# Four graph and expert layers on one core: bias vectors as bf16 parts, the weight ring ahead of the dispatch, choice by logits, an adjacency normalisation in attention

## The chip, the cores and the metric

The kernel runs on one core of a Trainium2 chip. A core has a matrix engine (PE, with its weight loads shown apart as PEld), a vector engine (DVE), a scalar engine (ACT), a general engine (POOL) and a queue engine for transfers (SP); each takes its instructions in order, and they meet through semaphores. The metric is the device time of one execution in microseconds (us), taken as the median of several runs.

## The reference

Four layers, each a graph convolution and a mixture of experts, act on 625 nodes with 512 features and 10,000 edges. Each half adds its result to x, and reads the normalised x:

```python
x = x + _L0_gnn_ref(_layernorm(x), edge_index, ...)   # mean over neighbours, two products, batch norm
x = x + _L0_ffn_ref(_layernorm(x)[None], ...)         # attention, then 8 experts of 128 hidden, all weighted
x = x + _L1_gnn_ref(_layernorm(x), edge_index, ...)   # two rounds of attention over the edges
x = x + _L1_ffn_ref(_layernorm(x)[None], ...)         # top 2 of 8 experts, 1024 hidden
x = x + _L2_gnn_ref(_layernorm(x), edge_index, ...)   # bases, mixed by weights of each node
x = x + _L2_ffn_ref(_layernorm(x)[None], ...)         # 8 experts of 128 hidden, two weights not zero
x = x + _L3_gnn_ref(_layernorm(x), edge_index, ...)   # one normalised convolution, gelu
x = x + _L3_ffn_ref(_layernorm(x)[None], ...)         # top 2 of 8 gated experts, 1536 hidden
```

What the change touches in it: an expert's output is `h @ W2[e] + b2[e]`, weighted by the node's gate, so the biases of all experts add `comb @ b2` (nodes x 8 times 8 x 512). Layer 1 chooses by logits and takes a softmax over the two chosen ones; layer 3 takes a softmax over all eight, the top two of it, and divides both by their sum. Layers 2 and 3 weigh each edge with `dinv[src] * dinv[dst]`, where `dinv` is one over the root of the degree.

## The kernel before

Nodes lie in NT = 5 tiles of T = 125, features in KD = 4 groups of 128. Matrix products are in float32, which the profile shows as two records each; one-hots and counts are fp16. The framework places instructions on each engine's queue and adds waits by its own reading of the dependencies; tiles of a closed pool give their addresses to the next, whose writers then wait for the last users.

**Setup.** The matrix of edge counts is a product of one-hots: for each of 80 groups of 125 edges, DVE makes `src` and `dst` (L911, L913) and PE adds five products into `ps_a` (L916). It is done in three parts of 27, 27 and 26 groups. After each part ACT casts `ps_a` to integers `v` (L929), DVE splits them into digits (L934, L936), and in the first part the layer norm `xn` is computed (L277 to L303), turned to features `xnT` (L328, L226), and added to x by POOL (L946). The four `ps_a`-sized PSUM buffers are shared by all this. The expert vectors `b2s` (8 rows of 3 x 512) and two rows of constants `cbs` are loaded there by SP.

**Weights** come as chunks of 1 MB, issued by SP at L206: three at a time through `take` for most stages, and through a ring of 11 in the routed experts (three of `take`'s buffers, five of a pool opened there, three of the pool `T` of feature tiles).

**Small experts** (layers 0 and 2, `small_experts`): two experts' hidden parts (`ahead`, `ps_mf`, L359) go first, then the bias product (`expert_bias`: five transposes L479, copies of the turned weights L481 and L482, five products `ps_eb` L486, each added to x by DVE), and then, expert by expert, the next hidden part and the outputs (`ps_eo`, L496).

**Routed experts** (layers 1 and 3): the normed rows go to DRAM (`rows_out`, L511), logits give the two chosen experts of each node (`top2`), `dispatch` gives every chosen pair a place in a block of 128 rows of one expert, by prefix sums on PE and one-hot products, and so the list `node` of the rows of each block (L584) and later the `gate` of each row (L615). `routed` then opens the ring, gathers each block's rows by an indirect DMA on POOL (`fetch`, L667), turns them (L674), multiplies by the expert's first weights (`ps_h`; L1170 in layer 1, L1335 in layer 3), turns the hidden part (L688) and multiplies by the second weights (`ps_y`, L697); the result is weighted (L703) and added into DRAM by an indirect DMA (L705). A list `fill` gives small tasks to slip between the units: in layer 1 the bias product, the keeping of x, and the steps of `normalise` (L1195), which turns the edge counts into the normalised adjacency that layers 2 and 3 use. The ring's first 11 chunks are asked for in `refill()`, after the dispatch in the program.

**Attention of layer 1** runs two rounds `l`; each makes q, k and v from three chunks of weights and then calls `attention`, where ACT, DVE and POOL work on 625-wide rows of scores (L796 to L860).

**Layer 2's convolution** adds, in the product `pr` of each of five node tiles, the rows `cbs` by a two-row product with ones.

Of the kernel before, what the change touches and what calls it, by code (L numbers as in the profile page):

```python
# [10 lines left out]
F32 = mybir.dt.float32  # L11
# [7 lines left out]
P = 128  # L19
# [133 lines left out]
def kernel(  # L153
# [29 lines left out]
    b2s = const.tile([34, 3, D], F32, name="b2s")  # L183
    cbs = b2s[32:34, 0, :]
# [287 lines left out]
    def expert_bias(comb, b2):  # L472

        cT = small.tile([P, NP], F32, tag="lg_T", name="cT", bufs=1)[:E]

        def turned():
            ps = pstile("ps_eb")
            for t in range(NT):
                nc.tensor.transpose(ps[:E, t // 4, t % 4 * T:(t % 4 + 1) * T], comb[:, t, :],  # L479
                                    ident[:T, :T])  # L480
            nc.scalar.copy(cT[:, :4 * T], ps[:E, 0, :4 * T])  # L481
            nc.vector.tensor_copy(cT[:, 4 * T:N], ps[:E, 1, :T])  # L482

        def added(t):
            ps = pstile("ps_eb")
            nc.tensor.matmul(ps[:T, 0, :], cT[:, t * T:(t + 1) * T], b2, start=True, stop=True)  # L486
            nc.vector.tensor_add(x[:, t, :], x[:, t, :], ps[:T, 0, :])

        return [turned] + [lambda t=t: added(t) for t in range(NT)]
# [24 lines left out]
    def dispatch(layer, o12, weight, w0, per):  # L514


        with tc.tile_pool(name=f"{layer}d", bufs=1) as dp:
# [12 lines left out]
            for s in range(NT):  # L530
                nc.tensor.matmul(tot, ones16, mask[:, s, :], start=(s == 0), stop=(s == NT - 1))
            gt = dp.tile([P, E, 4], F32, tag="gt", name="gt")
# [30 lines left out]
            ohp = dp.tile([T, 2 * NT, B], BF16, tag="ohp", name="ohp")  # L563
            ohb = dp.tile([T, 2 * NT, NB], F32, tag="ohb", name="ohb")
            nc.vector.tensor_tensor(ohb, blk[:T, None, :].to_broadcast([T, 2 * NT, NB]),
                                    bcast(at[:, 1, :], NB), op=OP.is_equal)
            nums = dp.tile([T, 2 * NT, NB, 2], BF16, tag="nums", name="nums")
            num = number.rearrange("p c t i -> p (c t) i")
            for i in range(2):
                nc.vector.tensor_mul(nums[:, :, :, i], ohb, bcast(num[:, :, i], NB))  # L570
            ps = pstile("ps_id")
            for n in range(2 * NT):
                nc.vector.tensor_scalar(ohp[:, n, :], place[:T, :], at[:, 0, n:n + 1], None,
                                        op0=OP.is_equal)
                nc.tensor.matmul(ps[:, 0, :2 * NB], ohp[:, n, :],
                                 nums[:, n].rearrange("p b i -> p (b i)"), start=(n == 0),
                                 stop=(n == 2 * NT - 1))
            one = dp.tile([P, NB], F32, tag="one", name="one")
            nc.vector.tensor_reduce(one, ps[:, 0, :2 * NB].rearrange("p (b i) -> p b i", i=2),
# [170 lines left out]
    def small_experts(src, comb, b1, b2, hpool, ln):  # L750
# [12 lines left out]
        for e in range(2):  # L763
            ahead(e)
# [615 lines left out]
```

## Time and profile before

| what | us |
|---|---|
| median of three runs | 1726.1 |
| lowest and highest | 1724.55, 1726.1 |
| the profiled execution | 1723.04 |
| its span | 1721.1 |
| PE busy in it | 1528.4 |
| DVE busy | 676.1 |
| ACT busy | 357.8 |
| POOL busy | 235.5 |

The page gives the share of busy time of each engine in 40 equal slices of the span, then the transfers, then the chain of work that ended last, then the costliest groups of instructions. A digit of the slices is tenths; the row PEclk is the clock granted to PE in tenths of full speed, and its mean over the span is 0.936. Where a line is followed by a bracket, it says how long the engine was idle before it and what released it. A group of one line and one form reads like this: the line, the engine, the operation, the tiles written and read, partitions x elements of each, how many, busy time and mean duration in ns, and the idle time before:

```profile
L1335 PE MATMUL ps_h<-ring,xgT 128*128 128x512 f32 x624 | 274.8, 595 | 0.8 <-DVE xgT L226 0.8
L825 POOL TENSOR_SCALAR s<-s,rs 125x625 f32<-125x625 f32 (+4 forms) x120 | 103.2, 875 | 294.0 <-DVE rs L822 269.9
```

The first is the largest product of the kernel, 624 records that hardly ever wait. The second is an operation that is often idle for the engine ahead of it.

### The profile page before, as it was taken

The page shows a single profiled execution, that of the slowest core. Times are in us where ns is not written, and L with a number is a line of the kernel's source. Part 1 is how long each engine was busy: PE and PEld are TensorE (multiplying, and loading weights), DVE is VectorE, ACT ScalarE, POOL GpSimd, SP SyncE. Part 2 cuts the span into 40 slices and gives each one's busy share as a digit, 9 for nine tenths or more (in the row PEclk, how much of TensorE's full clock was granted, in tenths as well). Part 3 has the DMA queues.
Part 4 walks back from the last instruction along what each step waited for, and adds up shares of the span by engine and source line. Part 5 has one row for each costly group of instructions (what it writes and reads, how often), then busy time and mean ns, then how long its engine had stood idle before and what let it go on. Part 6 is the DMA issues. An engine that isn't in the chain of part 4 may idle for free.

```text
span 1721.1 us, 15559 instructions
## 1 busy us (share of the span) xinstructions
PE 1528.4 (89%) x5642; PEld 861.3 (50%) x5642; DVE 676.1 (39%) x1738; ACT 357.8 (21%) x680; POOL 235.5 (14%) x254
## 2 busy tenths in 40 slices
PE   7996999989897989846999969698759999999997
PEld 5774466555555656533444436354534444444443
DVE  9824562451974168466122225635331111111110
ACT  1102362011661046311111115301211000000100
POOL 2010042010540034101111112001000000000000
PEclk8998999999999989977999989799869999999998
DMA  3000200011001100136889731011258888869871
GB/s 135 16 28 25 73 1 25 31 68 53 22 1 49 49 26 1 40 112 234 302 270 342 256 87 73 25 49 49 102 217 299 301 309 304 307 244 359 311 265 50
DMA packets 40142, 237.12 MB, mean 138 GB/s; under 512 B 4779, under 2 KB 4907, under 8 KB 14299
## 3 DMA queue, kind: packets, MB, share of 16 engines
q1 hardware_dynamic: 30705, 214.80, 33.7%
q0 software_dynamic: 6608, 15.99, 4.1%
q10 hardware_dynamic: 2746, 5.25, 1.0%
q8 instruction: 48, 0.79, 0.2%
q14 instruction: 35, 0.29, 0.1%
HBM read 246.11 MB, written 14.26 MB: 151 GB/s over the span
## 4 chain that ended last, share of the span: by engine, by line
PE 70%; DVE 12%; issue 10%; DMA 4%; ACT 2%; POOL 1%; SPq 0%; POOLq 0%; ACTq 0%; DVEq 0%
PE ps_mf L359 17%; PE ps_y L697 9%; PE ps_h L1335 9%; PE ps_mn L367 7%; PE ps_h L1170 5%; PE ps_s L796 4%; PE ps_eo L496 4%; PE ps_o L860 3%; DMA sumsL<-slots,node 3%; PE ps_p L839 3%; PE ps_tr L328 2%; DVE ln_st L277 1%; DVE s L802 1%; PE ps_t L688 1%; DVE dst L913 1%
## 5 line engine op out<-in xcount | busy, mean ns | idle before, releaser
L1335 PE MATMUL ps_h<-ring,xgT 128*128 128x512 f32 x624 | 274.8, 595 | 0.8 <-DVE xgT L226 0.8
L697 PE MATMUL ps_y<-ring,hT 128*128 128x512 f32 x536 | 239.2, 593 | 0.9 <-issue 0.9
L1335 PEld LDWEIGHTS ps_h<-ring,xgT 128*128 128x128 f32 x624 | 118.7, 191 | 147.9 <-issue 145.3
L697 PEld LDWEIGHTS ps_y<-ring,hT 128*128 128x128 f32 x536 | 97.6, 190 | 103.9 <-issue 103.0
L825 POOL TENSOR_SCALAR s<-s,rs 125x625 f32<-125x625 f32 (+4 forms) x120 | 103.2, 875 | 294.0 <-DVE rs L822 269.9
L705 POOL DMA_INDIRECT sumsL<-slots,node x27 | 42.6, 1578 | 469.3 <-DVE slots L703 358.6
L1338 ACT ACTIVATE g<-ps_h 128x512 f32<-128x512 f32 x39 | 23.3, 597 | 395.6 <-PE ps_h L1335 364.5
L1170 PE MATMUL ps_h<-ring,xgT 128*128 128x512 f32 x224 | 103.2, 609 | 2.1 <-ACT xgT L234 1.3
L807 ACT ACTIVATE s<-s,mn 125x626 f32<-125x626 f32 (+4 forms) x120 | 87.2, 743 | 49.3 <-DVE mn L802 49.1
L802 DVE CUSTOM_DVE_ANT_0 s<-ps_s,mask 125x626 f32<-125x626 f32 (+4 forms) x120 | 82.6, 718 | 29.0 <-PE ps_s L796 27.8
L796 PE MATMUL ps_s<-kT,qT 64*125 64x313 f32 (+4 forms) x416 | 86.4, 466 | 2.8 <-DVE mn L802 2.8
L328 PE MATMUL ps_tr<-ident,xn 125*128 125x125 f32 x140 | 30.2, 398 | 62.6 <-DVE ln_nb L300 49.1
L226 DVE COPY hT<-ps_t 128x512 f32<-128x512 f32 x26 | 18.0, 692 | 171.5 <-PE ps_t L688 171.5
L1340 DVE TENSOR_TENSOR h<-ps_h,g 128x512 f32<-128x512 f32 x39 | 26.8, 686 | 147.9 <-ACT g L1338 147.9
L839 PE MATMUL ps_p<-ident,s 125*125 125x125 f32 x432 | 65.8, 293 | 14.0 <-POOL s L825 11.7
L359 PE MATMUL ps_mf<-xT,w 128*128 128x313 f32 x256 | 69.7, 434 | 6.6 <-ACT xT L402 6.6
L839 PEld LDWEIGHTS ps_p<-ident,s 125*125 125x125 f32 x432 | 53.9, 194 | 40.0 <-POOL s L825 28.6
L1170 PEld LDWEIGHTS ps_h<-ring,xgT 128*128 128x128 f32 x224 | 43.6, 196 | 57.5 <-issue 53.8
L817 DVE SCALAR_TENSOR_TENSOR s<-s,cnt 125x626 f32<-125x626 f32 x80 | 67.3, 863 | 9.9 <-ACT s L807 9.9
L496 PE MATMUL ps_eo<-w,h 128*125 128x512 f32 x160 | 70.6, 592 | 0.0
L860 PE MATMUL ps_o<-pT,v 125*64 125x375 f32 (+2 forms) x448 | 60.1, 413 | 9.0 <-DVE mn L802 4.2
L916 PE MATMUL ps_a<-dst,src 125*128 125x313 f16 x400 | 58.0, 309 | 6.9 <-DVE dst L913 5.3
(345 smaller groups left out, 1994.8 us busy)
## 6 DMA issues: line engine op xcount, KB each, us to landing
ring<-in_weights SPq DMA_DIRECT2D x195, 1024.0 KB
w<-in_weights SPq DMA_DIRECT2D x27, 1024.0 KB
rows_hbm<-xn ACTq DMA_DIRECT2D x2, 1120.0 KB
sumsL<-x ACTq DMA_DIRECT2D x2, 1120.0 KB
out<-sumsL SPq DMA_DIRECT2D x1, 1250.0 KB
x<-in_x SPq DMA_DIRECT2D x1, 1120.0 KB
x<-sumsL SPq DMA_DIRECT2D x5, 224.0 KB
rows<-in_rows SPq DMA_DIRECT2D x1, 1052.0 KB
```

The costliest lines, as they stand in the source:

```text
L359: nc.tensor.matmul(ps[:, half, :HC], w, r[:, half * HC:(half + 1) * HC], start=(n == 0), stop=(n == last))
L367: nc.tensor.matmul(ps[:T, 0, :width], src[:, k, t * T:(t + 1) * T], w[:, k, :width], start=(k == 0), stop=(k == KD - 1 and extra is None))
L496: nc.tensor.matmul(ps[:T, 0, :], h[:, t * T:(t + 1) * T], w, start=(f == 0), stop=(f == len(blocks) - 1))
L697: nc.tensor.matmul(ys[b][:, 0, :], hT[:, j, :], ring[n % RING][:, j, :], start=(c == 0 and j == 0), stop=(c == nch - 1 and j == 3))
L796: nc.tensor.matmul(ps[hh][:T, i, :w], qT[rr, b, t * T:(t + 1) * T], kT[rr, b, i * w:(i + 1) * w], start=True, stop=True)
L802: nc.vector.tensor_tensor_reduce(s[:, hh, :nb * w].rearrange("p (a c) -> p a c", a=nb), ps[hh][:T, :nb, :w], mask[:, t, :nb * w].rearrange ...
L807: nc.scalar.activation(s[:, hh, :nb * w], s[:, hh, :nb * w], AF.Exp, bias=mn[:, hh:hh + 1], scale=-1.0, accum_out=sm[:, hh:hh + 1] if caus ...
L825: nc.gpsimd.tensor_scalar(s[:, hh, :w], s[:, hh, :w], rs[:, hh:hh + 1], 1.0, op0=OP.mult, op1=OP.mult)
L839: nc.tensor.transpose(pp[:T, hh, j * T:(j + 1) * T], s[:, hh, j * T:(j + 1) * T], ident[:T, :T])
L860: nc.tensor.matmul(po[rr, 0, o:n * T], v[:, j, h * DH:(h + 1) * DH], pT[:, hh, j, o:n * T], start=(j == 0), stop=(j == nk - 1))
L1170: nc.tensor.matmul(ps[:, 0, :], xgT[:, k, :], w1[:, k, :], start=(k == 0), stop=(k == KD - 1))
L1335: nc.tensor.matmul(ps[:, i, :], xgT[:, k, :], w[i][:, k, :], start=(k == 0), stop=(k == KD - 1))
```

## The change

1. `b2s` becomes 72 rows of bf16: each float32 is held as three bf16 parts which add up to it, in three groups of rows, and each group is loaded in copies. `cbs` becomes six rows in the same way. A new helper `parted` builds both in setup: transfers on ACT's queue, then copies and masked activations on ACT and subtractions on POOL. The weights `comb` are split in three parts as well (`parts`, on POOL), so that one bf16 product of 72 rows stands for the float32 product of 8 rows. In `small_experts` the bias steps come inside the expert loop, after the third hidden part. In layer 2's convolution the two-row product becomes a six-row bf16 product.
2. `routed` makes the choice and the dispatch itself. Its pools are opened and the ring's 11 chunks are asked for before them, and the first two gathers are issued as soon as `node` is there.
3. The choice goes by logits in both routed layers, and the weight of a pair comes from the exponent of their difference (`choose`, `weigh`), computed after the prefix sums.
4. The number of a row is one fp16 value and not two bf16 parts, so that `nums` has 17 columns and not 34, and one reduction goes.
5. `normalise` is called in layer 1's second attention round, two steps after each group of q, k and v, and no longer in the routed experts' fill.

```diff
-    b2s = const.tile([34, 3, D], F32, name="b2s")
-    cbs = b2s[32:34, 0, :]
+    b2s = const.tile([9 * E, 3, D], BF16, name="b2s")
+    cbs = const.tile([6, D], BF16, name="cbs")
...
-    def expert_bias(comb, b2):
-        cT = small.tile([P, NP], F32, tag="lg_T", name="cT", bufs=1)[:E]
+    def expert_bias(comb, layer):
+        cT = small.tile([9 * E, NP], BF16, tag="cT", name="cT", bufs=1)
+        rest = stile("eb_r")
+        part = small.tile([T, NT, E], BF16, tag="eb_p", name="eb_p")
+        c9 = small.tile([T, NT, 3, 3, E], F32, tag="c9", name="c9", bufs=1)
+
+        def parts():
+            nc.gpsimd.tensor_copy(rest, comb)
+            for i in range(3):
+                nc.gpsimd.tensor_copy(part, rest)
+                if i < 2:
+                    nc.gpsimd.tensor_sub(rest, rest, part)
+                for j in range(3):
+                    nc.gpsimd.tensor_copy(c9[:, :, j, i, :], part)
...
-                nc.tensor.transpose(ps[:E, t // 4, t % 4 * T:(t % 4 + 1) * T], comb[:, t, :],
-                                    ident[:T, :T])
-            nc.scalar.copy(cT[:, :4 * T], ps[:E, 0, :4 * T])
-            nc.vector.tensor_copy(cT[:, 4 * T:N], ps[:E, 1, :T])
+                nc.tensor.transpose(ps[:9 * E, t // 4, t % 4 * T:(t % 4 + 1) * T],
+                                    c9[:, t].rearrange("p j i e -> p (j i e)"), ident[:T, :T])
+            nc.scalar.copy(cT[:, :4 * T], ps[:9 * E, 0, :4 * T])
+            nc.scalar.copy(cT[:, 4 * T:N], ps[:9 * E, 1, :T])
...
-            nc.tensor.matmul(ps[:T, 0, :], cT[:, t * T:(t + 1) * T], b2, start=True, stop=True)
+            nc.tensor.matmul(ps[:T, 0, :], cT[:, t * T:(t + 1) * T], b2s[:, layer, :], start=True,
+                             stop=True)
...
+    def choose(lg):
+        m1, m2, o12 = top2(lg)
+        g12 = small.tile([T, 2, NT], F32, tag="g12", name="g12")
+        def weigh():
+            nc.vector.tensor_sub(g12[:, 1], m2, m1)
+            nc.scalar.activation(g12[:, 1], g12[:, 1], AF.Exp)
+            nc.vector.tensor_scalar(g12[:, 0], g12[:, 1], 1.0, None, op0=OP.add)
+            nc.vector.reciprocal(g12[:, 0], g12[:, 0])
+            nc.vector.tensor_mul(g12[:, 1], g12[:, 1], g12[:, 0])
+        return o12, g12, weigh
...
-            for i in range(2):
-                nc.vector.tensor_mul(nums[:, :, :, i], ohb, bcast(num[:, :, i], NB))
+            nc.vector.tensor_mul(nums, ohb, bcast(number.rearrange("p c t -> p (c t)"), NB))
...
-            nc.vector.tensor_reduce(one, ps[:, 0, :2 * NB].rearrange("p (b i) -> p b i", i=2),
-                                    axis=AX.X, op=OP.add)
...
             nc.vector.scalar_tensor_tensor(node, one, -1.0, free, op0=OP.add, op1=OP.add)
+            fetch(node)
...
-            refill()
+            while brought["n"] < RING:
+                bring(brought["n"])
+                brought["n"] += 1
+            o12, g12, weigh = choose(lg)
+            gate, whose = dispatch(layer, o12, g12, weigh, w0, per, first_rows)
...
-        for step in expert_bias(comb, b2):
-            step()
         for e in range(E):
             if e + 2 < E:
                 ahead(e + 2)
+            for step in bias[3 * e:3 * e + 3]:
+                step()
...
+    def parted(dst, src, n, pool):
+        rows3, width = dst.shape
+        per = rows3 // 3
+        full = pool.tile([rows3, width], F32, name=f"full{n}")
+        for g in range(rows3 // n):
+            nc.scalar.dma_start(full[g * n:(g + 1) * n], src)
...
+        for j in range(2):
+            nc.scalar.copy(dst, full)
+            nc.scalar.activation(part, dst, AF.Copy, scale=off[:, j:j + 1])
+            nc.gpsimd.tensor_sub(full, full, part)
+        nc.scalar.copy(dst, full)
...
-                nc.sync.dma_start(b2s[:E], b2_in)
-                nc.sync.dma_start(cbs, cb_in)
+                parted(b2s.rearrange("p l d -> p (l d)"), b2_in, E, setup)
+                parted(cbs, cb_in, 2, setup)
...
         for l in range(2):
+            if l == 1:
+                normalise()
...
-            pr = mm_nodes(xnT, wres, t, extra=(ones[32:34, :T], cbs))
+            pr = mm_nodes(xnT, wres, t, extra=(ones16[:6, :T], cbs))
...
-    pr = softmax8(node_logits(xnT, vec("L3_ffn_router_w"), None, "lg"))
-    m1, m2, o12 = top2(pr)
...
-    node, gate, whose = dispatch("L3", o12, g12.rearrange("p c t -> p (c t)"), W_L3, 9)
+    lg = node_logits(xnT, vec("L3_ffn_router_w"), None, "lg")
```

## The prediction

> **What bounds the kernel now.** I read the page's shares and slices first, then the chain that ended last, then stretches of it.
>
> ```profile
> PE   7996999989897989846999969698759999999997
> DVE  9824562451974168466122225635331111111110
> PEclk8998999999999989977999989799869999999998
> PE 70%; DVE 12%; issue 10%; DMA 4%; ACT 2%; POOL 1%; SPq 0%; POOLq 0%; ACTq 0%; DVEq 0%
> ```
>
> PE is the bound: 89% busy and 70% of the chain. A slice is 43 us. The first, one with PE at 4, and some with a clock of 6 to 8 tenths are where something else decides, and these are where the change works. In the long stretches of 9 (expert blocks) it alters nothing, so I forecast only at the seams.
>
> Rows of the chain, then stretches (length; busy time of PE, PEld, DVE, ACT, POOL; clock; DMA share; GB/s):
>
> ```profile
> 299.73 6.53 PE ps_eb L486 x10
> 786.47 5.24 DMA slots<-rows_hbm,node
> 1112.96 7.38 PE ps_eb L486 x10
> 1272.42 7.72 DMA slots<-rows_hbm,node
> ```
>
> ```profile
> 298.00:306.20 8.20, 7.42 (x18) 2.62 (x16) 3.03 (x5) 1.23 (x2) 4.96 (x1) 0.75 0.00 1
> 1111.50:1120.30 8.80, 8.02 (x17) 2.85 (x15) 3.03 (x5) 1.23 (x2) 0.00 (x0) 0.67 0.01 2
> 1120.30:1126.80 6.50, 6.50 (x17) 4.42 (x17) 0.69 (x1) 0.00 (x0) 0.00 (x0) 0.66 0.00 0
> ```
>
> The 8-row fp32 bias products (L486) stand on the path three times, and with them the clock is about two thirds, also over the full-size matmuls just after; it is 1.00 in the stretch that follows each (311 to 316, 1126.8 to 1131). The two gathers are waited for bare.
>
> **1. Setup (`parted`): costs +9.** Setup's start, from the timeline:
>
> ```profile
> 27.46 7.38 POOL L946 TENSOR_TENSOR x<-x,xn 125x512 f32<-125x512 f32 x5 [17.92 <-DVE ln_nb L300]
> 29.24 1.55 DVE L934 TENSOR_SCALAR acc<-v 125x626 int32<-125x626 int32 x1
> 32.34 0.42 ACT L929 CAST v<-ps_a 125x313 int32<-125x313 f32 x1 [2.74 <-DVE acc L936]
> 32.82 1.10 PE L328 MATMUL ps_tr<-ident,xn 125*128 125x125 f32 x4 [2.06 <-ACT v L929]
> 36.29 24.00 PE L916 MATMUL ps_a<-dst,src 125*128 125x313 f16 x166 [1.59 <-DVE xnT L226]
> ```
>
> Until 25 DVE paces (20.00 us busy in 5 to 25, the one-hots); between the first and second part of the edge count PE waits for the norm, and resumes at 36.29. The change puts 12 DMA issues, a table load, six copies and four activations on ACT, and four subtractions on POOL, into this. Loads end at about 18 (DMA row), so `b2s`'s copies start about 11 to 17. What waits on ACT's in-order queue is behind all of them: the norm's root, `xn`, the casts `v`, so PE and DVE wait with it. The order built of the changed program has ACT: copies, two activations, root of the norm, two `v`, copies, activations, two `xn`, third copies, third `v`, `xnT`. Sizes: ACT copies 512 columns in 0.58 (rows of 128x512), so 1536 in about 1.7, and POOL adds 125x512 in 1.27 (L1133), so 1536 in about 3.8 and the small one in 1.27.
>
> Here a rule speaks against the change. Row: DVE's 125x626 int32 op takes 1.55 while POOL adds, and 0.48 at 55.9 and later with POOL idle. The Trainium skill, page "SBUF — State Buffer", section "🔬 SBUF: two separate sides", says that the pair which VectorE and GpSimd share is locked exclusively for a whole instruction. By the row alone (three times slower) the first subtractions cost 5.1 × 2/3 = 3.4; by the rule all 5.1. I take 5.1, since DVE is full there: norm's root at 28.6, `v` to 31, ACT's second pieces (1.7+0.6)×2 = 4.6 to 35.6, POOL's second long subtraction to about 37.7 to 39.5 (five row additions of 7.38 share its queue), ACT's third pieces 2.3 to about 42, third `v`, then as now 36.29 − 32.34 = 4 to PE's restart: 45.5 to 46.5. Forecast +9. Ends: 0 (all under the one-hots) and +12.
>
> **2. Layer 0's experts: −2.** POOL builds nine columns of parts with 15 small ops (a copy of 32 columns takes POOL 0.21, so 0.2 to 0.3 each: 3 to 4.5). They queue behind the mask (L1080), 11.24 us from 291.72 to 302.96, so they end at 306 to 307.5. Now experts' output begins at 311.88. The two `ahead`s no longer have the bias between them and end about 302.6; then PE does the third `ahead` (5.8 us at the slow clock, 3.5 at full), so the parts are covered but for about 1 us. Bias after: five transposes and five bf16 products. A full fp32 128x512 product is 3.44/4 = 0.86; fp16 ones of 313 columns (ps_a) take 0.14, so 512 take about 0.23, five 1.2. Removed: 6.53 + about 1 of clock; returned: about 2.5 with transposes, and up to 3 of waiting for POOL. I take −2, ends −4 and +1.
>
> **3. Layer 1's attention: +1.2.** The normalisation (four reciprocals of 1.06, three products of 0.81, one of 0.49, five pairs of 0.35 and 0.87: 13.1 us of DVE) goes, by the built order, into the first round's k/v stage and not the second's. v's products run 410.89 to 428.2, DVE has two evictions there (417.95, 424.82), the first score op is 429.60. Most lies under those 17 us; DVE comes free about 430.8. Ends 0 and +2. Attention is paced by ACT, DVE and POOL from there.
>
> **4. Layer 1's dispatch: −1.7.** Before the node numbers at 786.0 one of two products (0.59) goes; I count −0.55 with the reduction against conversions. The gather: 5.24 now, with the remainder of the ring fetched at the same instant:
>
> ```profile
> 787.30 44.37 SPq L206 DMA_DIRECT2D ring<-in_weights  x12
> 1271.90 37.72 SPq L206 DMA_DIRECT2D ring<-in_weights  x12
> 1272.42 1.04 POOL L667 DMA_INDIRECT slots<-rows_hbm,node  x1 [78.02 <-DVE gate L615]
> ```
>
> The window 787 to 800 has DMA at 0.92 and 357 GB/s. In the change ring chunks 3 to 7, 9 and 10 wait only for buffers of the stage before, so 5 MB or so (15 us at that rate) run under the 12 to 15 us of the choice. The fastest gathers of `slots` take 4.0 to landing: −1.2. If the ring is still in flight, 0. On SP the moved issues now stand ahead of the load of the routing table, which is wanted only by the overflow blocks; one that waits for a buffer holds nothing earlier. On POOL both fetches (1 us each) move ahead of the new `parts`, which therefore reach PE's fill about 4 us later, with PE busy on `ps_h` meanwhile.
>
> **5. Layer 1's first blocks: −5.5.** The bias products among them take 1.98 at 800.36 and 2.83 at 805.89, 4.8; bf16 1.2: −3.5. A wait of 1.28 for ACT's xgT and a first `ps_h` of 5.24 against the usual 3.4 should partly go, since DVE loses the fill (8.07 of 9 us in 800 to 809): −2. Ends −3 and −8.
>
> **6. Layer 2's conv: −1.9.** The 2-row fp32 `cbs` product becomes bf16: 0.6 of 6.84 per node tile in the first three; later tiles are DVE-bound. Ends −3 and 0. A root table now loads at layer 2's start; under a DMA wait: 0, uncovered 1.28.
>
> **7. Layer 2's experts: −7.3.** From the bias transposes (1111.48) to expert output (1126.80) are 15.3 us. Left: the third `ahead` at full clock, about 4; transposes and ten copies 2; bias later 1.2. POOL is idle and `comb` ready at about 1110. 15.3 − 8 = 7.3. The gain is half the products (7.38 → 1.2) and otherwise the clock. The second place where a page is weighed: "TensorE: Matmul & The Clock Gate", Part 1, has a cold clock follow from idle windows. The row contradicts that: PE is busy 8.02 of 8.80 at 0.67. By the page the clock would stay whatever form the product has, and only about −4.5 remain; by the row the thin fp32 products bring it down. I take the row. Ends −4 and −9.
>
> **8. Layer 3's dispatch: −6.1.** Choosing by logits takes the softmax's six ops out of the path (1259.92 to 1261.35): −1.43. Node numbers −0.6. The fetch now waits for the gate (the row above), 0.6 to 0.9 after node: −0.6. Its gather, 7.72 beside the ring, to about 4.2: −3.5. The new weights' exponent comes after the rank products, off the path. Ends −2.5 and −8.
>
> Sum: 9 − 2 + 1.2 − 1.7 − 5.5 − 1.9 − 7.3 − 6.1 = −14.3. The profiled execution took 1723.04 (span 1721.1), so 1708.7; the median shown is 3.06 higher, and I forecast on that: 1726.1 − 14.3 = **1711.8**.
>
> **Rivals.**
> A, *setup hides*: `parted`'s work runs under the one-hots and the lock costs only +0.5. For: ACT is idle till 23.50. Against: the third `v` stands behind two POOL rounds. 1711.8 − 8.5 = 1703.3.
> B, *gathers and clock don't recover*: ring still in flight (4 loses 1.2, 8 loses 3.5), clock stays low behind the new products (7 loses 2.8, 5 loses 2, 2 loses 1). For: the page on the clock; the gather is a scattered transfer whose own latency was never seen below 4.0. Against: DMA is idle for most of the 40 us before either dispatch. 1711.8 + 10.5 = 1722.3.
> C, *setup outweighs all* (slower): POOL's subtractions on 72x1536 run at the mask's rate (11.24 for 3130 columns, 5.5 each) with DVE locked out, and ACT's in-order queue, which waits for the last pieces' DMA, holds the norm's root, `xn` and `v` behind it. It decides from 14.3 + 9 = 23.3 us; for 27 the landing would have to be some 18 us later than the row. Against: loads end at 18. Then 1726.1 + 4 = 1730.
> That the change does not do what it says: the normalisation already does not go where the text puts it (step 3); that is in the sum.
>
> **Chances.** Forecast 0.58 (own range 1706 to 1718), A 0.18, B 0.13, C 0.11. A measurement here tells about 0.2%, 3.4 us, from nothing: the whole of C slower or near nothing (0.08 slower, 0.03 same); B splits, 0.08 faster and 0.05 same; the others are faster. So faster 0.84, same 0.08, slower 0.08. The range takes A's own lower side and reaches B: 1700 to 1724.
>
> **What would show it.** Step 1: PE's restart of `ps_a` at about 46 where it was 36.29, DVE rows of about 3.8 us beside a POOL subtraction. 2 and 7: bias rows of about 0.2 each and a clock near 1.00 after them. 4 and 8: gathers at about 4 us with ring chunks all issued before. 3: first score op at about 430.8 plus the shift. Wrong if the restart is before 38 or after 55, if the clock stays near 0.67 behind bf16 products, or if gathers stay over 5.

## The result, and the profile after

The changed kernel takes 1712.0 us (median of 6 runs, 1711.1 to 1717.04) against 1725.37 for the kernel before (median of 6): a ratio of 0.9928, with a 95% interval from 0.9915 to 0.9941, or 13.4 us less. The forecast was 1711.8.

The slices of the page after, to be laid beside those of before:

```profile
PE   5997999889898899954999996698859999999997
DVE  8834453362984338554212224845241111111110
PEclk8898999999999899976999998899969999999999
PE 56%; issue 10%; DVE 9%; DMA 4%; ACT 2%; POOL 1%; ACTq 0%; SPq 0%; POOLq 0%; DVEq 0%
```

The first slice of PE has fallen from 7 to 5: setup has become longer. The long stretches of 9 at the end are the same, only earlier. The shares of the chain add up to 82% here and to 99% before, so they are not compared; PE itself is busy 1514.5 us in place of 1528.4.

The profiled execution of this run was its slowest, 1717.04 us. The second one below, of the same kernel, took 1714.16 (span 1712.1). I compare that one with the profile before (1723.04, span 1721.1), mark by mark; each mark is the start of a group of PE's instructions.

| mark | before | changed | shift | the stage gave | forecast |
|---|---|---|---|---|---|
| last group of edge counts | 62.42 | 74.48 | +12.1 | +12.1 setup | +9 |
| layer 0, second expert output | 320.39 | 332.91 | +12.5 | +0.5 experts | −2 |
| layer 1, end of attention (`ps_tn`) | 749.31 | 761.95 | +12.6 | +0.1 | +1.2 |
| layer 1, first gathered rows turned | 791.85 | 802.08 | +10.2 | −2.4 dispatch | −1.7 |
| layer 1, first `ps_y` | 816.54 | 822.49 | +6.0 | −4.3 first blocks | −5.5 |
| layer 2, norm turned | 1032.90 | 1039.89 | +7.0 | +1.0 | 0 |
| layer 2, convolution's result turned | 1088.64 | 1094.60 | +6.0 | −1.0 | −1.9 |
| layer 3, `ps_tn` | 1237.04 | 1233.81 | −3.2 | −9.2 experts of layer 2 | −7.3 |
| layer 3, first gathered rows turned | 1280.28 | 1270.02 | −10.3 | −7.0 dispatch | −6.1 |
| layer 3, second hidden products | 1297.92 | 1288.87 | −9.1 | +1.2 | 0 |

The stages sum to −9.0, and the medians of the two kernels stand 12 to 13 us apart. The profiled execution before was 1.2 us below the median of the runs beside which this one was timed, and the changed one 2.1 above its own, which makes the other 3.3 us. Part of them is in the first row: setup is the same in six profiled executions (the two here and those of four amended kernels below), and in them the last group of counts starts between 72.49 and 74.48, the last being the one in the table. In seven executions without the preparation in setup it starts between 62.02 and 63.82. The means are 73.3 and 62.9, so setup costs 10.4 us on average, and the table has it high.

Setup in the timeline of the changed kernel (first execution), rows in order of start (start, duration, engine, line, operation, tiles):

```profile
28.48 4.73 POOL L934 TENSOR_TENSOR full<-full,part 72x1536 f32<-72x1536 f32 x2 [14.19 <-ACT part L933]
...
30.76 1.33 DVE L968 TENSOR_SCALAR src<-nodes,ef 125x640 f16<-125x640 f16 x1
...
32.02 1.23 DVE L252 TENSOR_TENSOR rs_v<-rs_v,rs_r 125x5 f32<-125x5 f32 x1
...
39.41 4.96 POOL L934 TENSOR_TENSOR full<-full,part 72x1536 f32<-72x1536 f32 x2
...
40.30 2.95 DVE L968 TENSOR_SCALAR src<-nodes,ef 125x640 f16<-125x640 f16 x1
...
45.00 0.41 ACT L986 CAST v<-ps_a 125x313 int32<-125x313 f32 x1
...
46.98 24.92 PE L973 MATMUL ps_a<-dst,src 125*128 125x313 f16 x168 [0.25 <-DVE xnT L226]
```

Three DVE operations that take 0.38, 0.16 and 0.38 elsewhere (medians of their lines) stand at 1.33, 1.23 and 2.95 while POOL subtracts, and each ends when POOL's instruction does. Not every operation is held: the copies of `xnT` out of PSUM take 0.67 beside POOL and 0.65 to 0.68 elsewhere. The third cast follows ACT's third copies, which follow the second subtraction, and PE resumes at 46.98.

Layer 0, one row of the kernel before and then the same execution of the changed one; after them two windows of the changed kernel (length; busy time and count of PE, PEld, DVE, ACT, POOL; clock; DMA share; GB/s):

```profile
289.81 8.60 PE L359 MATMUL ps_mf<-yT,w 128*128 128x313 f32 x32
...
301.73 12.81 PE L359 MATMUL ps_mf<-yT,w 128*128 128x313 f32 x48
...
303.64 11.27 POOL L1131 TENSOR_SCALAR mask<-cnt 125x3130 bf16<-125x3130 f32 x1 [5.22 <-ACT cnt L234]
314.97 0.22 POOL L480 COPY eb_r<-sm_p 125x40 f32<-125x40 f32 x1
...
318.32 1.26 PE L491 MATMUL ps_eb<-ident,c 125*72 125x125 f32 x5 [3.77 <-POOL c L486]
```

```profile
316.00:321.30 5.30, 2.32 (x8) 1.51 (x9) 0.34 (x1) 0.74 (x2) 2.00 (x11) 0.66 0.00 0
321.30:327.30 6.00, 6.00 (x12) 2.46 (x11) 3.95 (x6) 0.00 (x0) 0.00 (x0) 0.73 0.00 0
```

PE waits 3.77 us for the parts that queue behind POOL's mask, and the clock is down for much of the six busy microseconds that follow. It fell during the wait: windows of half a microsecond have it at 1.00 up to 317.5 and at 0.50 from 318, before the first of the new products at 320.24. The gathers, from the chain of waits:

```profile
801.61 3.60 DMA slots<-rows_hbm,node
...
1269.45 3.33 DMA slots<-rows_hbm,node
```

Both are shorter than any gather of the trace before (4.0 at least).

### The profile page after: what moved, and what is told of

The parts are those of the page before. It is cut to its first block, busy times and chain, and to the rows that moved or that the text cites. A ratio compares the mean times of both kernels' runs of the same rounds, so it can differ in the third digit from the quotient of the medians.

```text
span 1715.1 us, 15597 instructions
## 1 busy us (share of the span) xinstructions
PE 1514.5 (88%) x5622; PEld 858.1 (50%) x5622; DVE 676.1 (39%) x1720; ACT 369.6 (22%) x694; POOL 256.4 (15%) x309
## 4 chain that ended last, share of the span: by engine, by line
PE 56%; issue 10%; DVE 9%; DMA 4%; ACT 2%; POOL 1%; ACTq 0%; SPq 0%; POOLq 0%; DVEq 0%
PE ps_mf L359 11%; PE ps_y L728 9%; PE ps_h L1385 9%; PE ps_h L1252 5%; PE ps_eo L509 4%; PE ps_mn L367 3%; PE ps_s L831 3%; DMA sumsL<-slots,node 3%; PE ps_o L895 3%; PE ps_p L874 2%; PE ps_t L719 1%; DVE ln_st L277 1%; PE ps_tr L328 1%; DVE s L837 1%; PE ps_lg L421 1%
## 5 line engine op out<-in xcount | busy, mean ns | idle before, releaser
L328 PEld LDWEIGHTS ps_tr<-ident,xn 125*128 125x128 f32 x140 | 25.6, 216 | 80.8 <-issue 61.1
```

Source lines behind the costliest of these rows:

```text
L328: nc.tensor.transpose(ps[:, 0, k * T:(k + 1) * T], src[:, t, k * P:(k + 1) * P], ident[:T, :T])
```

## The experiments

Each kernel was timed in turn with the kernel before on the same chip; the ratios are to it. The intervals are 0.0024 to 0.0033 wide, 4 to 6 us, so a difference of 3 us between two amended kernels is read from the single runs as well. The differences below are of medians; the kernel before has medians from 1724.06 to 1725.37 in the five sets of runs, so between kernels of different sets up to 1.3 us can be the set.

**The changed kernel again** (no edit).

> The changed kernel once more, unaltered, to see how its profiled execution stands to its median: the first one took 1717.04 us where the median is 1712.0. If the 5 us lie in one stage (a slow gather, a slow clock), this profile shows that stage shorter and a span near 1710; if they are spread, it shows no stage that differs by over 1 us. The ratio to the kernel before should be 0.9928 again.

1712.1 us, 0.9926 (0.9912 to 0.9939). The span of the profiled execution is 3.0 us shorter than the first. The difference is in one place, ACT's queue in layer 1; first execution, then second:

```profile
781.60 3.11 ACTq L524 DMA_DIRECT2D rows_hbm<-xn  x2
```

```profile
782.13 0.87 ACTq L524 DMA_DIRECT2D rows_hbm<-xn  x2
```

In the first, the second of the two issues waited some 2.2 us, the copies of `xnT` behind it came late, and PE then made the logits at half clock (3.97 us against 2.33). The expectation of the run that moves the rows, below, puts this down to a transfer of the ring. The trace doesn't bear that out: in both executions the weights' queue moves nothing between 778 and 795 us, and in the first only the rows themselves are moved from 782 to 788. The time of the two issues differs between the other kernels too: 1.11 in the kernel before, and from 0.87 to 2.00 in the amended kernels that leave them in place. What the second one waits for stays open. The forecast had not priced such a wait, and of the two executions only one has it.

**Setup: the parts built later** (in layer 0's convolution).

```diff
-                parted(b2s.rearrange("p l d -> p (l d)"), b2_in, E, setup)
-                parted(cbs, cb_in, 2, setup)
...
         rc = pool.tile([P, NP], F32, name="rc")
+        parted(b2s.rearrange("p l d -> p (l d)"), b2_in, E, pool)
+        parted(cbs, cb_in, 2, pool)
```

> The parts of the bias vectors are built after the edge counts (in layer 0's convolution), nothing else changes. My theory: the preparation in setup costs 11.5 us of the changed kernel (end of the edge-count products 74.6 before, 86.0 after), by POOL's subtractions that hold DVE and by ACT's queue in front of the third cast; so the restart of the counts is back near 36.3 and the time falls by 10 to 12 us against the changed kernel (1700 to 1702), ratio to before about 0.986. Rival: the preparation is wanted anyway and collides with something in layer 0's convolution (ACT, DVE held by POOL), so that less than half of it comes back (1706 or more).

1703.34 us, 0.988 (0.9865 to 0.9895): 8.8 us less than the changed kernel. In its trace the last group of counts starts at 62.70, as before (62.42), so all of setup's loss is back. The profiled span is 12 us shorter (1700.3 against 1712.1), but that sets the fastest of four runs against the slowest of five; the medians give 8.8, less than the 10 expected, and the average of setup above is 10.4. The rival (under half) falls. POOL's subtractions now lie at 103 and 110 us, beside PE's float32 products.

**Setup: the subtractions on DVE.**

```diff
-            nc.gpsimd.tensor_sub(full, full, part)
+            nc.vector.tensor_sub(full, full, part)
```

> The changed kernel with the four subtractions of the setup on DVE in place of POOL; ACT's transfers, copies and activations stay. My theory: POOL's subtractions cost twice, DVE stands still beside them and ACT's third copies wait for them; on DVE they take about 1.6 and 0.6 us a pair, so of the 11.5 us in setup 3 to 6 come back (1706 to 1709). Rival: ACT's queue (copies and activations ahead of the norm and the casts) is the whole cost: no change (1711 to 1713).

1707.33 us, 0.9905 (0.989 to 0.992): 4.8 us less, within what the theory said. PE resumes at 40.77, 6.2 us ahead of the changed kernel. So about half of setup's loss comes of having the subtractions on POOL: the time for which they hold DVE, and the wait of ACT's third copies for them. The other half was not taken apart. ACT's copies and activations are in it, and so are the subtractions themselves, which DVE now makes: 2.35 us for the first pair and 4.49 for the second, beside POOL's row additions.

**Layer 0: the parts ahead of the mask.** The mask takes a zero that is computed from the last part, and so cannot start before it.

```diff
-        bias = expert_bias(comb, layer)
-        bias.pop(0)()
...
+        bias = expert_bias(gate, 0)
+        c9 = bias.pop(0)()
+        zero = pool.tile([T, 1], F32, name="zero")
+        nc.gpsimd.tensor_scalar(zero, c9[:, NT - 1, 2, 2, E - 1:], 0.0, 1.0, op0=OP.mult,
+                                op1=OP.mult)
         mask = pool.tile([T, NT, NP], BF16, name="mask")
-        nc.gpsimd.tensor_scalar(mask, cnt, 0.0, NEG, op0=OP.is_equal, op1=OP.mult)
+        nc.gpsimd.tensor_scalar(mask, cnt, zero, NEG, op0=OP.is_equal, op1=OP.mult)
```

> Layer 0's mask of the next layer (11.3 us of POOL) is made to wait for the 15 small operations that split the gates, instead of standing ahead of them; nothing else changes. My theory: PE idles 3.8 us for the parts at 314.5 and then runs at two thirds of its clock for 6 us more, so the time falls by 3.8 for the wait and about 1.7 for the clock, 5.5 us in all (1706 to 1707), and the clock stays at 1.00 over the first expert output. Rival: the clock falls with the bias products themselves, then only 3.8 us come back; or the gates come too late in any case (under 1 us).

1704.51 us, 0.9886 (0.9871 to 0.9901): 7.6 us less, where 5.5 were expected. Its timeline and window:

```profile
314.00 0.65 PE L499 MATMUL ps_eb<-b2s,cT 72*125 72x512 bf16 x2 [0.80 <-ACT cT L494]
314.48 4.46 PE L510 MATMUL ps_eo<-w,h 128*125 128x512 f32 x10
```

```profile
316.00:321.30 5.30, 5.30 (x17) 2.98 (x16) 3.41 (x5) 0.00 (x0) 0.52 (x1) 1.00 0.00 0
```

The first expert output takes 4.46 us in place of 6.15 and the clock is 1.00. From the last group of counts to the second expert output it is 251.5 us, against 258.4 in the changed kernel: 6.9. The wait is 3.8 of it and the clock 2.7, and not 1.7 as expected, since the transposes and the first bias products gain from it too (0.70 and 0.65 in place of 1.26 and 1.11). The bf16 products themselves do not bring the clock down; the pause before them did.

**The rows after the turned rows.**

```diff
+        xnT = to_features(xn, "xnT")
         for part, hbm in by_node(rows_hbm):
             nc.scalar.dma_start(hbm, xn[part])
-        return to_features(xn, "xnT")
+        return xnT
```

> In both routed layers the two transfers of the normed rows to DRAM are asked for after the turned rows are copied out by ACT, not before; nothing else changes. My theory: in layer 1 the second of them waits on ACT's queue about 2.4 us for a ring transfer that was asked for early, the copies behind it come late, PE idles 2.6 us and then makes the logits at half clock (3.97 us where it was 2.33): so the time falls by 2 to 3.6 us (1708.5 to 1710). Rival: the rows then land too late for the first gather, which grows by as much: no change. Layer 3 has no such wait and doesn't move.

1709.16 us, 0.9913 (0.9897 to 0.9928): 2.9 us less. The interval overlaps that of the changed kernel, but the runs don't: 1708.36 to 1710.2 against 1710.96 to 1714.16. From the end of attention to the logits the profile shows 21.27 us, against 21.72 in the second execution above, which had no long wait, and the first hidden product at 5.17 us in place of 6.57. So the two issues alone cost some 0.5 us at that place, 1.4 is the clock, and the wait of the first execution comes on top where it falls. The expected 2 to 3.6 thus came true in part by luck: they were worked out from a wait that most executions do not have.

**The ring and the first gathers after the dispatch again.**

```diff
+        nodes = []
+        o12, g12, weigh = choose(lg)
+        gate, whose = dispatch(layer, o12, g12, weigh, w0, per, nodes.append)
         with tc.tile_pool(name=f"{layer}w", bufs=1) as more,
...
-            while brought["n"] < RING:
-                bring(brought["n"])
-                brought["n"] += 1
-            o12, g12, weigh = choose(lg)
-            gate, whose = dispatch(layer, o12, g12, weigh, w0, per, first_rows)
+            refill()
+            fetch(0)
+            fetch(1)
```

> The changed kernel with the choice and the dispatch standing again ahead of the opening of the ring's buffers, so that the ring is completed and the first gathers are issued only after the dispatch, as before; all else is as changed. My theory: the first gathers grow again beside the ring (3.6 to about 5.2 in layer 1, 3.3 to about 7.7 in layer 3) and layer 3's is issued 0.6 later, 6 to 7 us lost; the wait of the rows on ACT's queue in layer 1 goes (2 to 3.6 us gained); so 3 to 4 us slower than the changed kernel (1715 to 1716). Rival: what the early ring gives to the gathers it takes back by that wait and by a colder clock, no difference (1711 to 1713).

1714.77 us, 0.994 (0.9924 to 0.9957): 2.7 us more, the runs overlapping (1712.85 to 1720.52). The two gathers, from the chain:

```profile
796.86 3.90 DMA slots<-rows_hbm,node
...
1265.19 6.50 DMA slots<-rows_hbm,node
```

In layer 3 the gather is 6.50 us beside the ring's transfers, where the changed kernel has 3.30; that part of the theory holds, with 3.2 for the 4.4 expected. In layer 1 it is 3.90, which looks as if the ring did not matter there. But the ring was not beside it. The traces give what the weights' queue moved while each gather was under way:

| kernel | layer 1: gather, weights moved | layer 3: gather, weights moved |
|---|---|---|
| before | 5.24 us, 0.88 MB | 7.72 us, 2.37 MB |
| changed, second execution | 3.69 us, none | 3.30 us, none |
| ring after the dispatch | 3.90 us, 0.34 MB | 6.50 us, 1.46 MB |

In layer 1 of this run the ring is asked for 1.16 us after the gather (0.83 in the kernel before), and all but 0.03 MB of the 0.34 comes in the last 0.8 us. So the run does not decide for layer 1. In all six gathers more weights go with a longer gather, which is what the forecast said of both layers; it is not proof, since a longer gather also leaves more time for weights to pass.

**The bias product over 128 rows, in the kernel before.**

```diff
-    b2s = const.tile([34, 3, D], F32, name="b2s")
+    b2s = const.tile([P, 3, D], F32, name="b2s")
+    nc.gpsimd.memset(b2s, 0.0)
...
-        cT = small.tile([P, NP], F32, tag="lg_T", name="cT", bufs=1)[:E]
+        cT = small.tile([P, NP], F32, tag="lg_T", name="cT", bufs=1)
+        nc.gpsimd.memset(cT, 0.0)
```

> The kernel before, with its float32 bias product made over 128 rows, 120 of them zero, in place of 8; same number of products, same order, one clearing of the turned gates added on POOL. My theory: products over 8 rows bring the matrix engine's clock down and keep it there; with 128 rows the clock is near 1.00 in layer 0 and layer 2 over the bias products and the hidden part after them, each falls from about 13 to 9 us, and the time falls by 6 to 10 us (1716 to 1719, ratio about 0.995). Rival: the clock goes down by the gaps in PE's work before (0.8 us for the turned gates), and the number of rows doesn't matter: no change (1723 to 1726).

1715.52 us, 0.9942 (0.993 to 0.9954): 9.6 us less than the kernel before, in which nothing was changed but the 120 added rows (zero in `cT`, so that they add nothing) and their clearing on POOL. Two rows of the kernel before, then timeline and windows of this run:

```profile
299.73 6.53 PE L486 MATMUL ps_eb<-b2s,cT 8*125 8x512 f32 x10 [0.78 <-ACT cT L481]
306.20:311.00 4.80, 4.80 (x14) 3.35 (x14) 0.69 (x1) 0.00 (x0) 0.00 (x0) 0.71 0.01 3
```

```profile
301.70 4.56 PE L488 MATMUL ps_eb<-b2s,cT 128*125 128x512 f32 x10 [0.78 <-ACT cT L483]
```

```profile
298.00:306.20 8.20, 7.42 (x26) 3.88 (x25) 3.02 (x5) 1.23 (x2) 6.93 (x1) 1.00 0.00 1
306.20:311.00 4.80, 4.80 (x19) 3.29 (x18) 0.69 (x1) 0.49 (x1) 0.00 (x0) 1.00 0.02 3
```

The wait before the products is the same 0.78 us, PE's busy time in the window is the same 7.42, and the clock is 1.00 in place of 0.75. Ten products take 4.56 us where ten with 8 rows took 6.53. So it is the small number of rows that brought the clock down here, not a gap. The next run shows the limit of this: four or six such products bring it down in some places only.

**The bias in float32 over 8 rows, in the changed kernel.** The parts in setup and of the gates fall away; `b2s`, `cbs` and `expert_bias` are those of the kernel before, in the new places.

```diff
-                parted(b2s.rearrange("p l d -> p (l d)"), b2_in, E, setup)
-                parted(cbs, cb_in, 2, setup)
+                nc.sync.dma_start(b2s[:E], b2_in)
+                nc.sync.dma_start(cbs, cb_in)
```

> The changed kernel with the bias vectors and the conv's constants in float32 again: 8-row float32 products, no parts in setup and none of the gates, loads on SP; the placing of the bias steps in the expert loop and all else stays. My theory: the bf16 parts win about 8 us in layer 2's experts, 4 in layer 1's blocks and 1 to 2 in layer 2's convolution, and pay 11.5 us in setup, while layer 0 is about even; so the whole of this part is worth about 1 to 2 us and this kernel takes 1711 to 1715. Rival: the parts win more in the clock than they cost, 1718 or more; or they are a loss, 1707 or less.

1718.27 us, 0.996 (0.9948 to 0.9973): 6.2 us slower than the changed kernel, so my estimate (1711 to 1715) was too low and the rival holds. In its profile the account is even: 12.1 us gained in setup, 12.0 lost from there to layer 3. But that profiled execution was the fastest of six, 1714.53, and the others took 1717.62 to 1720.45; what they add was not seen. In layer 0 the trace has

```profile
303.90 2.38 PE L489 MATMUL ps_eb<-b2s,cT 8*125 8x512 f32 x4 [0.78 <-ACT cT L484]
306.21 7.50 PE L500 MATMUL ps_eo<-w,h 128*125 128x512 f32 x10
...
317.86 2.83 PE L489 MATMUL ps_eb<-b2s,cT 8*125 8x512 f32 x6
320.62 4.56 PE L500 MATMUL ps_eo<-w,h 128*125 128x512 f32 x10
```

Four products over 8 rows are followed by a slow output and six by one at full speed. In layer 2 it is the other way round: 4.56 us after four, 6.25 after six. Ten in a row brought the clock down both times; what decides for a few is not shown. So the bf16 parts as they stand are worth about 6 us by the medians, with setup's cost against them.

**The normalisation back in the fill.**

```diff
             if l == 1:
-                normalise()
...
-            fill = list(rest(o12, g12)) + [keep]
+            fill = list(rest(o12, g12)) + [keep] + list(more_fill)
```

> The changed kernel with the normalisation put back among the small tasks of layer 1's routed experts, after the keeping of x; all else is as changed. My theory: its place hardly matters: in the attention it lies wholly under the products of v (the first score comes at the same distance with it and without it), and among the experts DVE has room, so it costs at most the 1 to 2 us by which it delays DVE's copies in the first blocks (1712 to 1714). Rival: it was what made the first blocks slow, and 3 us or more come back on (1715 or more).

1708.69 us, 0.9914 (0.9901 to 0.9928): 3.4 us less by the medians, against both theories. By the ratios it is 2.1 to 2.4, and the intervals overlap, so the size is not certain. Attention and first blocks do not differ from the changed kernel (shifts −1.16 and −1.07 where setup stood at −1.19). Layer 2 begins 1.5 us earlier: no root table is loaded there, and DVE's order of the small operations of the norm is the old one. In the changed kernel the table's load itself is over before the root is wanted (1032.16 to 1033.44, root at 1036.72), but the built order puts the reciprocal of the first three tiles behind the second group's statistics, and the first normed tile comes at 1039.20, 2.5 us after its root, where it is 1.9 us with the fill; the rest is a later landing of x (DVE waits 1.28 us for it, against 0.68). The clock after it gives another 1 us.

**All three amendments.**

> The three amendments in one: the bias parts are built in layer 0's convolution, the mask waits for the gates' parts, the rows go to DRAM after the turned rows. Alone they took 8.8, 7.6 and 2.9 us from the changed kernel's 1712.1. My theory: they lie in three different stages and add, so 1692 to 1694, ratio to before about 0.982. Rival: two of them share something (the clock, or POOL's queue) and a third of the sum is lost, 1699.

1692.35 us, 0.981 (0.9797 to 0.9823). The three alone took 8.8, 7.6 and 2.9 from 1712.1, which leaves 1692.8: they add.

**All three, and the normalisation in the fill.**

> The kernel with all three amendments and, beside them, the normalisation back in the routed experts' fill. Alone the last took 3.4 us from the changed kernel, by the start of layer 2, where no root table has to be loaded any more and DVE's order of the norm's small operations is the old one. My theory: that stage has nothing to do with the other three, so it adds: 1692.35 less 3.4, 1688 to 1690, ratio to before about 0.979. Rival: the 3.4 us were the clock's phase and not that stage, and little of them is found again: 1691 to 1693.

1693.31 us, 0.9808 (0.9795 to 0.9822): nothing more. In the profile layer 2 begins 0.7 us earlier relative to the end of layer 1, and the next two stages take 0.3 and 0.2 us more. So of the 3.4 us a small part was that stage and the rest does not repeat here; it is not shown what it was.

**All three, with idle transposes in the dispatch.**

```diff
+            for i in range(14):
+                nc.tensor.transpose(ps[:, 1, 256:256 + P], ident, ident)
             weigh()
...
+            for i in range(10):
+                nc.tensor.transpose(ps[:, 1, 256:256 + P], ident, ident)
             gate = small.tile([P, NB], F32, tag="gate", name="gate")
```

> The kernel with all three amendments, and in both dispatches 14 transposes of the identity without use after the prefix sums and 10 after the gates' products, so that PE is not idle while DVE makes the node numbers and while the first gather is under way. My theory: the half clock of the first hidden products (16.7 us for 32 records in layer 3 where 13.8 is full speed, 6.4 for 8 in layer 1 where 3.4 is) comes from those idle stretches, so 2.5 to 3 us come back in each: 1686 to 1688. Rival: the clock needs more than this, or doesn't follow from idleness: 1692, or slower by up to 1 us where the idle transposes delay the products behind them.

1699.18 us, 0.9853 (0.9838 to 0.9868): 6.8 us slower than without them. The comparison `gt` reads the bank that the transposes write, and waits for them: 2.56 us idle in layer 3's dispatch, where it waited 0.61, and 2.55 for 0.82 in layer 1's. That is the edit's fault and explains some 4 us of the loss; by the marks the two dispatches are 2.9 and 4.2 us longer. But the clock did not come either:

```profile
1242.00:1246.00 4.00, 3.81 (x24) 3.41 (x23) 1.23 (x8) 0.68 (x1) 0.00 (x0) 0.50 0.00 0
...
1250.00:1255.00 5.00, 4.10 (x29) 3.22 (x28) 2.11 (x12) 0.00 (x0) 1.88 (x2) 0.50 0.08 17
...
1258.00:1262.00 4.00, 3.92 (x5) 1.85 (x6) 0.03 (x1) 0.00 (x0) 0.52 (x1) 0.50 0.28 88
```

PE is 95% and 82% busy with transposes and small products and stays at 0.50; the hidden products then start at half clock all the same, 16.85 us for 32 records. This does not show that such work can't raise the clock. The busy stretches were short, under 4 us and with 3.8 us of idleness between them, and the hidden products themselves, PE full, ran 5.8 us here before the clock rose (4.7 with the three amendments alone). A longer stretch was not tried.

## Why the forecast was right, and where it was not

The total was right to 0.2 us by the medians; its terms were less right than that, and errors of both signs met in it. The forecast was also set on 1726.1, the median of three runs, where six give 1725.37: a fall of 14.3 was forecast and 13.4 was measured. The direction and the size are the forecast's; the 0.2 is luck.

1. **Setup** was forecast by its mechanism: ACT's queue, POOL's lock, the third cast. PE's restart was forecast at 45.5 to 46.5 and is 46.98 and 47.60 in the two executions. Two errors met in it: the third cast was due at about 42 and came at 45.00, since the second subtraction waits behind three row additions until 39.41, and from the cast to the restart it took 2.0 where 4 were put. The term taken from it, +9, was too small: the restart is 10.7 and 11.3 late, and the counts after it add another 0.8. Of the two readings of the shared port the lock was the right one: the three operations that met a subtraction did not end before it did. Moving the work (8.8 us) and moving the subtractions (4.8) confirm that the parts are the cost and that POOL's subtractions are about half of it; ACT's queue is read from the timeline, not tested alone.
2. **Layer 0's experts**: this is the step that failed. The parts came when forecast: in the first execution PE's wait for them ends at 318.32, that is at 306.4 without the 11.9 us by which the stage starts later, and 306 to 307.5 was the forecast. But PE was free too early. The forecast had two hidden parts end at about 302.6 and the third run on from there, so that only about 1 us of the wait would show. By the row of the kernel before two end at 298.4, and in the changed kernel it is all three that end at 314.54, or 302.6 without the 11.9. So 3.77 us showed, and what the sum did not have is that the pause costs the clock besides: 6.15 us for a stretch of 4.46, and 1.0 more in the products before it. The stage gave +0.5 in place of −2, and the amendment that takes the pause away brought 7.6.
3. **Attention**: +0.1 for +1.2; the normalisation lies under v's products, with or without it the first score comes at the same distance.
4. **Layer 1's dispatch**: −2.4 for −1.7 in the execution without the wait of the rows. In the one with it the stage lost 1.4 us (turned rows at 805.35, 13.5 late, after attention had been 12.1 late). The gather did shorten, to 3.6 and 3.7, below the 4.0 assumed, and the forecast's reason fits the bytes: 0.88 MB of weights moved beside it before, none now. No run took the ring away from it and nothing else.
5. **First blocks**: −4.3 for −5.5. The part for the products is there (0.43, 0.81 and 0.38 us stand for 4.8); the first `ps_h` at 6.4 to 6.6 in place of 5.33 takes some of it back: the clock is 0.53 in 807 to 813 of the first execution, where it was 0.66 in 793 to 799 before.
6. **Layer 2's conv**: −1.0 for −1.9, and +1.0 at its start, which the forecast had at 0 with 1.28 for an uncovered table load. The load was covered; the order of DVE that came with it was not. The product gives 0.7 in each of the five node tiles (6.14 us for 6.84), more than forecast, but PE then waits 9.52 us in place of 8.19 for DVE's norm, and the transposes and first products take 1.2 more at a colder clock.
7. **Layer 2's experts**: −9.2 for −7.3, just past the end of the range given to it (−9). The forecast's own terms leave 7.2 of the 15.3 us and not the 8 that it took off, so they say −8.1; and the products are most of the gain (7.38 to 0.65 ahead of the output, 0.8 later), the clock of the next hidden part 2.3, not half and half. The weighing of the page "TensorE: Matmul & The Clock Gate", Part 1, came out for the row: with 128 rows in place of 8 and the same gap, the clock stays up. The page's rule is not wrong for that: in layer 0 of the changed kernel the clock fell in an idle stretch of 3.77 us, as it says, and a pause taken away brought it back. The two causes stand side by side here.
8. **Layer 3's dispatch**: −7.0 for −6.1; the gather is 3.3 and the ring's early fill is worth 3.2 of the 4.4, by the run with the ring late. The softmax's 1.43 is there as well: from the logits' transposes to the ranks it is 4.24 us for 5.66. The single number of a row was not run alone. 1.2 comes back in the first hidden products, at a colder clock (16.71 us for 15.50).

What stays open: what the second issue of the rows waits for in some executions; why four or six products over 8 rows bring the clock down in one place and not in another; what the slower executions of the float32 variant add; where the 3.4 us of the normalisation in the fill came from beyond layer 2's start.

## What to carry to other kernels

Work that is prepared once costs what its engines' queues are holding at that moment: the same parts cost about 10 us in setup and next to nothing 75 us later. Where one instruction has to stand behind another in a queue, a value can hold it back, as the zero did with the mask. A few products over 8 rows can cost more in the clock of those that follow than in themselves (2.38 us for four of them, and 2.9 more in the output after them), so look at the clock's column in the windows before counting their microseconds, and pad or widen the rows. Before a run is taken to refute a cause, see in its trace that the cause was really taken away or brought in: the ring that was put after the dispatch did not meet the gather in layer 1. When a path is shortened, ask what stands in front of the next instruction in its queue, since most of the stages that disappointed here did so by an order of issue and not by work.

## What the runs showed of the hardware that was not expected

- Ten float32 products of 512 columns over 8 rows took 6.53 us at a granted clock of 0.75; over 128 rows, zeros included, 4.56 us at 1.00, and the stretch after them rose from 0.71 to 1.00. The whole kernel gained 9.6 us by adding zeros. At a clock of 1.00 the rows make no difference to the product itself: six over 8 rows took 2.83 us in the float32 variant, 0.47 each, and the ten over 128 rows 0.46 each.
- Transposes of the identity and small products, at 82 to 95% busy in windows of 4 and 5 us, left the clock at 0.50; but PE full of products over 128 rows also ran 2.8 us (layer 0 of the kernel before) to 5.9 us (layer 0 of the float32 variant) before the clock rose.
- Gathers of 128 rows took 3.3 to 3.7 us with no weights moved beside them, and 5.24, 6.50 and 7.72 us with 0.88, 1.46 and 2.37 MB.
- DVE operations of 0.15 to 0.4 us lasted 1.2 to 2.95 us when they met a POOL subtraction of 72x1536 or the small one after it, and ended with it; the two pairs of subtractions took POOL 4.7 and 5.0 us. Copies out of PSUM were not held.
